# A four-fold column order in a fused convolution-and-attention block, with three smaller edits

## The chip, the cores and the metric

The kernel runs on one core of one Trainium2 chip. The time is the device time of one execution in microseconds. Before the change the median of three runs was 2451.59 us (2448.86 to 2452.62).

The core has five engines that run beside each other and wait for one another by semaphores: TensorE (PE, matrix products into PSUM), VectorE (DVE, arithmetic on one or two tensors), ScalarE (ACT, functions such as exp and SiLU, and copies), GpSimd (POOL, here small arithmetic, memsets and issuing transfers) and SyncE (SP, here only issuing transfers). PEld is PE's loading of weights. Each engine works its own list in order, so an instruction that waits holds up all that stand behind it. SBUF is the on-chip memory, PSUM the memory into which PE accumulates.

## The reference

Eight images x of 512 channels and 32 x 32 pixels, all in fp32:

```python
h = group_norm(x)                           # 32 groups
t = silu(bn(conv1x1(h, cv1_w)))             # 512 -> 512 channels
ys = [t[:, :256], t[:, 256:]]
for i in range(2):                          # two bottlenecks
    yi = ys[-1]
    z = silu(bn(conv3x3(yi, m_cv1_w[i])))
    q, k, v = conv1x1(z, m_qkv_w[i])        # 4 heads of 64 channels
    r = m_rw[i] + m_rh[i]                   # one term per column, one per row
    a = softmax(q.T @ (k + r) / 8)          # 1024 x 1024 per head
    z = silu(bn(conv1x1(a @ v, m_cv2_w[i])))
    ys.append(yi + z)
out = x + silu(bn(conv1x1(concat(ys), cv2_w)))   # 1024 -> 512 channels
```

Only the 3x3 convolution and the position term r depend on where a pixel lies. The 1x1 convolutions and the attention take the pixels in any order, as long as it is the same throughout.

## The kernel before, in words

Channels lie on the 128 partitions, pixels along the free axis. The images are worked in four pairs (the loop over p), a and b. For each pair the first bottleneck (n = 0) is done for a and b, then the second (n = 1), then the final 1x1 convolution for both; the first 1x1 convolution and the group norm of the next pair run in between. The last pair has no next one (more is false), and its last image takes a plain product (cv2) in place of the seven-product scheme (strassen).

A 3x3 convolution is done as a transform of tiles: four columns and four rows of output at a time. tiles_in (L422 to L485) makes the transformed input for one of three groups of rows i. It first combines rows into w_rows, which has 34 columns: the 32 of the image and a zero at each side (memsets L452 and L453 on POOL). It then combines columns. As four neighbouring columns belong to one tile, every column operation reads or writes every fourth element: d is the difference of columns two apart (L467), L470 to L474 take d by its place in a quad, L480 and L481 read w_rows at each fourth column. L483 and L484 finish the third output from the two tiles of L480 and L481. conv3x3 (L487 to L567) multiplies (L528), and in each of its six steps turns the products back: c_m on ACT (L533), c_t twice and c_e on DVE (L534 to L540), four operations that write each fourth column of c_r (L542 to L545), then sums over rows into z (L548 to L560) and SiLU (the helper at L398).

project_strassen (L704 to L800) makes q, k and v of one image in seven products. It adds r to k in add_r, as two DVE operations for each of four pieces, one with the column term broadcast over rows (L740), one with the row term (L741); the last two pieces are done by later() at the start of the attention. attention_fast (L802 to L976) runs 32 steps in four groups: logits on PE (L825), exp on ACT (L829), running sums on DVE (L843, L845), and the product with v on PE (L859). Other work is hung into it by the dictionary behind, keyed by group and pair of steps. The exponentials, the temporary tiles of project_strassen and tiles that tiles_in makes for the second bottleneck (v_new, stored to DRAM at L1551) share one ring of six buffers, tag "pt".

group_norm (L623 to L655) makes the norm of the next image in four stages inside the attention, at groups 1, 2, the middle of 2, and 3. Its last stage takes the reciprocal root on POOL (L599). Then, for the first pair (direct is true), POOL computes a shift and ACT applies scale and shift in eight pieces (L654); for later pairs DVE does it in four (L633).

strassen (L1084 to L1174) is the final 1x1 convolution. finish (L1131) takes one finished block: SiLU in place, an addition of x, which POOL's queue loaded ahead (residual, L1124 to L1129), on DVE (L1135), and a store from POOL's queue (L1136). The temporary tiles are a ring of four, tag "t".

The order of the work is not written out entirely: the framework places each instruction on its engine's list at the time at which its own estimate of costs has it ready, by program order among those that are ready; issue_after adds an order by hand. Transfers are placed on SP's and POOL's lists in the same way.

Of the kernel before, what the change touches and what calls it, by code (L numbers as in the profile page):

```python
# [47 lines left out]
ALU = mybir.AluOpType  # L48
# [13 lines left out]
def kernel(  # L62
# [112 lines left out]
    def load_bottleneck(n):  # L175
        nc.sync.dma_start(rw_sb[:, n], m_rw[n].rearrange("(k p) f -> p k f", p=P))
        nc.sync.dma_start(rh_sb[:, n], m_rh[n].rearrange("(k p) f -> p k f", p=P))
        nc.sync.dma_start(m2_sb[:, n], m_cv2_w[n].rearrange("(k p) o -> p k o", p=P))

# [157 lines left out]
    v_dram = [[tc.dram_tile([P, 2, 2 * P], F32, name=f"v{i}{cp}") for cp in range(3)] for i in range(NI)]  # L337
    y0_dram = [[tc.dram_tile([P, NM, HALF], F32, name=f"y0_{b}{h}") for h in range(NH)] for b in range(B)]
# [46 lines left out]
    def img2(ap):  # L385
        return ap.rearrange("p c (h w) -> p c h w", w=F)

# [6 lines left out]
    def stages(act, small, ps_big, ps_av, n_pt):  # L394
# [27 lines left out]
        def tiles_in(yp, put, is_=(0, 1, 2), ec=None):  # L422
# [16 lines left out]
            for i in is_:  # L439
# [23 lines left out]
                else:  # L463
                    stt(to[0], two(ec[1]), 0.25, two(g[:, :, 0]), ALU.mult, ALU.add)
                    stt(to[1], two(ec[0]), -4.0, two(g[:, :, 1]), ALU.mult, ALU.add)
                d = act.tile([P, 2 * NT * NM, F], F32, tag="acc", name="w_d", bufs=2)
                tt(d, e[:, :, 2 : F + 2], e[:, :, 0:F], ALU.subtract)  # L467
                quads = d.rearrange("p a (s j) -> p (a s) j", j=4)
                v05, v12, v34 = (put(i, cp) for cp in range(3))
                stt(  # L470
                    v05.rearrange("p c q -> p q c"), quads[:, :, 0:2], -4.0, quads[:, :, 2:4], ALU.mult, ALU.add
                )
                stt(v34[:, 0], quads[:, :, 1], 2.0, quads[:, :, 2], ALU.mult, ALU.add)
                stt(v34[:, 1], quads[:, :, 1], -2.0, quads[:, :, 2], ALU.mult, ALU.add)  # L474

                def each4(m):
                    return e[:, :, m : m + F - 3 : 4]

                ab = act.tile([P, 2, 2 * NT * NM, NT], F32, tag="h", name="w_ab", bufs=2)
                stt(ab[:, 0], each4(2), -4.0, each4(4), ALU.mult, ALU.add)  # L480
                stt(ab[:, 1], each4(1), -4.0, each4(3), ALU.mult, ALU.add)  # L481
# [5 lines left out]
        def conv3x3(n, vs, u_of, z, groups=G, summed=None):  # L487
# [10 lines left out]
            for oc in range(NM):  # L498
                dst = z[:, oc].rearrange("p g x -> p (g x)").rearrange("p (t r w) -> p r t w", r=4, w=F)
                for i in range(NI):  # L500
# [40 lines left out]
                    r = act.tile([P, 2, q, 4], F32, tag="acc", name="c3_r", bufs=2)  # L541
                    stt(r[..., 0], m[:, :, 2], -0.25, e[:, :, 0], ALU.mult, ALU.add)  # L542
                    stt(r[..., 1], m[:, :, 3], -0.5, m[:, :, 1], ALU.mult, ALU.add)
                    tt(r[..., 2], m[:, :, 0], m[:, :, 2], ALU.subtract)
# [78 lines left out]
        def group_norm(xts, on_act=False):  # L623
# [21 lines left out]
            if not on_act:  # L645
                yield apply(range(NX), gm, gr)
                return
# [1214 lines left out]
```

## Time and profile before

| | |
|---|---|
| median of three runs | 2451.59 us |
| profiled execution | 2449.15 us |
| its span, first to last instruction | 2447.6 us |
| PE busy | 2254.5 us (92%) |
| DVE busy | 1933.5 us (79%) |
| ACT busy | 1012.0 us (41%) |
| POOL busy | 178.4 us (7%) |
| mean granted PE clock | 0.97 |
| moved by transfers | 272.01 MB, mean 111 GB/s |

A row of a group reads: line, engine, operation, output and inputs by name, partitions x elements, count; then busy time in us and the mean of one in ns; then the engine's idle time just before them and what ended it. A row of a timeline reads: start in us, length in us, engine, line, what it is, and in brackets the idle time before it with what ended it. A row of waits reads: who, for whom, us in total, times, the longest.

The stages of a later pair, by start in us, for the second pair: 750 to 781 first 3x3 convolution; 804 to 862 attention of image a; 920 to 980 attention of b; 1003 to 1061 tiles and second 3x3 convolution; 1074 to 1131 and 1160 to 1218 the two attentions of the second bottleneck; 1218 to 1322 the final 1x1 convolution of both images.

### The profile page before, as it was taken

To read this page: it belongs to the slowest core of one execution; us is meant where nothing else is said; L and a number is where in the kernel's file an instruction comes from. 1 tells how busy PE (TensorE), PEld (TensorE's weight loads), DVE (VectorE), ACT (ScalarE), POOL (GpSimd) and SP (SyncE) were. 2 spreads that over 40 slices of the span, in tenths; PEclk is the share of its full clock that TensorE was granted. 3 is DMA by queue.
4 is the path that set the end of the run, shared out by engine and by line. 5 is a ranking of instruction groups with operands and counts; after the bars stand their busy time and mean duration, and the time that the engine had idled before them with its cause. 6 is when DMAs were issued, how large, how long until landed. Compare 5 with 4: busy or idle time off the path is not lost.

```text
span 2447.6 us, 40591 instructions
## 1 busy us (share of the span) xinstructions
PE 2254.5 (92%) x16378; PEld 1101.8 (45%) x16378; DVE 1933.5 (79%) x2766; ACT 1012.0 (41%) x1301; POOL 178.4 (7%) x409
## 2 busy tenths in 40 slices
PE   6698778899999999999999998989999996989998
PEld 2462333634347443654346443463444732363433
DVE  7987585987878879886896879898796878597653
ACT  4145244255413545246511455436521363425531
POOL 4101210000010000000011000000001000000002
PEclk9799889999999999999999999999999998999999
DMA  9531622621146141532036223351124502141113
GB/s 318 196 106 53 233 75 96 209 88 41 60 168 211 31 151 40 178 97 86 21 119 235 83 75 117 108 168 58 45 82 163 184 23 74 49 158 36 57 31 122
DMA packets 128644, 272.01 MB, mean 111 GB/s; under 512 B 34016, under 2 KB 63184, under 8 KB 127424
## 3 DMA queue, kind: packets, MB, share of 16 engines
q1 hardware_dynamic: 104368, 184.51, 23.6%
q0 software_dynamic: 24080, 84.82, 9.5%
q8 instruction: 131, 2.15, 0.4%
q14 instruction: 65, 0.53, 0.1%
HBM read 200.20 MB, written 69.07 MB: 110 GB/s over the span
## 4 chain that ended last, share of the span: by engine, by line
PE 63%; DVE 25%; issue 5%; DMA 3%; ACT 3%; POOL 1%; SPq 0%; DVEq 0%; POOLq 0%; ACTq 0%
PE av_ps L859 14%; PE l_ps L825 14%; PE c L1078 8%; PE c_new L1078 6%; PE p_ps L717 5%; PE m_ps L1058 4%; DVE acc L845 3%; PE c_ps L528 3%; PE ps L417 3%; PE x_ps L1189 2%; PE pv_ps L723 2%; PE s_ps L876 1%; DVE c_e L536 1%; DVE w_d L467 1%; PE p_ps L723 1%
## 5 line engine op out<-in xcount | busy, mean ns | idle before, releaser
L829 ACT ACTIVATE pt<-l_ps 128x1024 f32<-128x1024 f32 x512 | 496.4, 1025 | 370.2 <-PE l_ps L825 332.9
L845 DVE TENSOR_TENSOR acc<-acc,pt 128x1024 f32<-128x1024 f32 x384 | 469.7, 1223 | 97.5 <-ACT pt L829 73.7
L825 PE MATMUL l_ps<-q,kr 64*64 64x512 f32 x4096 | 493.3, 597 | 49.4 <-ACT pt L829 46.7
L859 PE MATMUL av_ps<-pt,vT 64*64 64x512 f32 x4096 | 494.3, 600 | 7.7 <-DVE z L867 6.6
L825 PEld LDWEIGHTS l_ps<-q,kr 64*64 64x64 f32 x4096 | 158.2, 134 | 323.3 <-issue 250.0
L859 PEld LDWEIGHTS av_ps<-pt,vT 64*64 64x64 f32 x4096 | 158.3, 135 | 286.8 <-issue 234.4
L528 PE MATMUL c_ps<-v_in,u 128*64 128x128 f32 x4320 | 245.9, 277 | 16.3 <-ACT c_m L533 16.3
L528 PEld LDWEIGHTS c_ps<-v_in,u 128*64 128x64 f32 x4320 | 242.9, 140 | 22.8 <-ACT c_m L533 17.4
L717 PE MATMUL p_ps<-t_z,sq 128*128 128x512 f32 x256 | 128.5, 619 | 19.4 <-DVE c_t L535 19.4
L1058 PE MATMUL m_ps<-z,m_sb 128*128 128x512 f32 x256 | 114.6, 600 | 8.9 <-DVE z L931 8.9
L533 ACT COPY c_m<-c_ps 128x512 f32<-128x512 f32 x48 | 28.0, 584 | 211.6 <-PE c_ps L528 83.8
L717 PE MATMUL p_ps<-z,sq 128*128 128x512 f32 x192 | 93.5, 618 | 17.2 <-ACT z L398 10.9
L843 DVE TENSOR_TENSOR acc<-pt 128x1024 f32<-128x1024 f32 x64 | 78.2, 1221 | 32.9 <-ACT pt L829 32.9
L931 DVE TENSOR_TENSOR z<-z,rs 128x512 f32<-128x512 f32 x64 | 44.1, 689 | 70.8 <-DMA rs<-r_dram 70.7
L398 ACT ACTIVATE t<-m_ps,bh,sh 128x512 f32<-128x512 f32 x64 | 47.0, 779 | 86.9 <-PE m_ps L1058 86.5
L1058 PEld LDWEIGHTS m_ps<-z,m_sb 128*128 128x128 f32 x256 | 48.7, 192 | 68.7 <-issue 56.8
L717 PEld LDWEIGHTS p_ps<-t_z,sq 128*128 128x128 f32 x256 | 45.4, 197 | 54.7 <-issue 52.3
L723 PEld LDWEIGHTS pv_ps<-sq,z 128*128 128x128 f32 x384 | 51.4, 200 | 37.8 <-issue 11.0
L723 PE MATMUL pv_ps<-sq,z 128*128 128x128 f32 x384 | 55.0, 288 | 13.3 <-DVE z L867 7.2
L467 DVE TENSOR_TENSOR w_d<-w_rows 128x1024 f32<-128x1024 f32 x48 | 58.8, 1225 | 3.6 <-DVE w_rows L462 0.5
L717 PEld LDWEIGHTS p_ps<-z,sq 128*128 128x128 f32 x192 | 34.2, 193 | 58.0 <-issue 35.2
L417 PE MATMUL ps<-x,w 128*128 128x512 f32 x128 | 57.0, 599 | 0.9 <-ACT y_half L398 0.9
(279 smaller groups left out, 3179.9 us busy)
## 6 DMA issues: line engine op xcount, KB each, us to landing
u<-u SPq DMA_DIRECT2D x135, 512.0 KB
sq<-sq SPq DMA_DIRECT2D x48, 384.0 KB
x_res<-in_x_dram POOLq DMA_DIRECT2D x63, 256.0 KB, 4.2
rs<-r_dram SPq DMA_DIRECT2D x120, 128.0 KB
x<-in_x_dram SPq DMA_DIRECT2D x28, 512.0 KB
y_in<-y SPq DMA_DIRECT2D x28, 512.0 KB
u<-u_new POOLq DMA_DIRECT2D x54, 256.0 KB, 2.9
v<-v_new POOLq DMA_DIRECT2D x36, 256.0 KB, 2.3
```

What stands on the lines that cost most here:

```text
L417: last_product[0] = nc.tensor.matmul(ps[:, half, :], w_of(k), rhs_of(k, half), start=(k == begin), stop=(k == end))
L467: tt(d, e[:, :, 2 : F + 2], e[:, :, 0:F], ALU.subtract)
L528: nc.tensor.matmul(to[o], us[cp][:, k, row, c, o], rhs, start=(k == 0), stop=(k == NM - 1),)
L717: nc.tensor.matmul(ps[:, o, :], w[:, o, :], rhs, start=not onto, stop=True, skip_group_check=onto)
L723: nc.tensor.matmul(v[:, ts(j, P)], rhs[:, ts(j, P)], w[:, 2, :], start=j == 0 and not onto, stop=True, skip_group_check=True,)
L825: nc.tensor.matmul(ps[kh * HD : (kh + 1) * HD, hd, :], kr[r, c, o : o + HD], q[r, c, ts(half, HALF)], start=True, stop=True,)
L829: exp = nc.scalar.activation(pt, ps, AF.Exp, scale=SCALE)
L843: return nc.vector.tensor_tensor(accs[g], pt[0], pt[1], ALU.add)
L845: ins = nc.vector.tensor_tensor(accs[g], accs[g], pt[i], ALU.add)
L859: nc.tensor.matmul(avs[g][hd * HD : (hd + 1) * HD, kh, :], vT[r, j, o : o + HD], pt[i][r, hd, :], start=(j == 0), stop=(j == NJ - 1),)
L1058: nc.tensor.matmul(pss[oc][:, half, :], m2_sb[:, n, k, ts(oc, P)], ao[:, k, ts(half, HALF)], start=(k == 0), stop=(k == NM - 1),)
L1078: nc.tensor.matmul(ps[:, o, :], w[:, k, ts(o, P)], rhs[part][:, c], start=(k == 0 and not onto), stop=(k == KB - 1), skip_group_check=onto,)
```

## The change

**Column order.** Between the first and the final 1x1 convolution the 32 columns of a row are stored by their remainder modulo four, remainder 3 first, eight of each. The first 1x1 convolution's SiLU and copies write that order (planes, natural), the final one's SiLU writes the natural order back (from_planes, by_slot). In tiles_in and conv3x3 each operation on every fourth column becomes one on runs of eight; L467 becomes two operations of half the size. The copies of L1199 into ypad are split in two.

**Position term.** r is summed once for each bottleneck by POOL at the start, stored in DRAM, and loaded on SP's queue into two "pt" tiles at each project_strassen; add_r has one addition.

**Residual.** In strassen, SiLU writes a fresh "t" tile, a transfer on POOL's queue adds x to it, and a second one stores it. The loads of x and the DVE additions go.

**Norm.** The last stage of group_norm is on POOL and ACT for all pairs.

**Last pair.** The tiles of image a's second convolution, made between projection and attention of b before, are made inside that attention, after the second pair of steps of groups 0, 1 and 2; their tiles take the tag "x" in place of "pt". In the plain cv2 the partial sum is added in place.

```diff
     def load_bottleneck(n):
-        nc.sync.dma_start(rw_sb[:, n], m_rw[n].rearrange("(k p) f -> p k f", p=P))
+        raw = act.tile([P, NM, F], F32, tag="t", name="rw_raw", bufs=4)
+        nc.sync.dma_start(raw, m_rw[n].rearrange("(k p) f -> p k f", p=P))
         nc.sync.dma_start(rh_sb[:, n], m_rh[n].rearrange("(k p) f -> p k f", p=P))
         nc.sync.dma_start(m2_sb[:, n], m_cv2_w[n].rearrange("(k p) o -> p k o", p=P))
+        nc.gpsimd.tensor_copy(planes(rw_sb[:, n]), natural(raw))
+        for c in range(NM):
+            for half in range(NH):
+                r = act.tile([P, ROWS, F], F32, tag="t", name="r_new", bufs=4)
+                nc.gpsimd.tensor_tensor(
+                    r, rw_sb[:, n, c].unsqueeze(1).to_broadcast([P, ROWS, F]),
+                    rh_sb[:, n, c, ts(half, ROWS)].unsqueeze(2).to_broadcast([P, ROWS, F]), ALU.add,
+                )
+                nc.gpsimd.dma_start(r_dram[n][c][:, ts(half, HALF)], r.rearrange("p h w -> p (h w)"))
...
+    def planes(ap):
+        a = ap.rearrange("p (h w) -> p h w", w=F) if len(ap.shape) == 2 else ap
+        return bass.AP(
+            tensor=a.tensor, offset=a[:, :, F - NT :].offset, ap=[a.ap[0], a.ap[1], [1, NT], [-NT, 4]]
+        )
+    def natural(ap):
+        a = ap.rearrange("p (h w) -> p h w", w=F) if len(ap.shape) == 2 else ap
+        return a.rearrange("p h (s j) -> p h s j", j=4)
+    def by_slot(ap):
+        a = ap.rearrange("p (h w) -> p h w", w=F) if len(ap.shape) == 2 else ap
+        return a.rearrange("p h (j s) -> p h j s", j=4)
+    def from_planes(ap):
+        a = ap.rearrange("p (h w) -> p h w", w=F) if len(ap.shape) == 2 else ap
+        return bass.AP(tensor=a.tensor, offset=a[:, :, 3:].offset, ap=[a.ap[0], a.ap[1], [-1, 4], [4, NT]])
...
-                d = act.tile([P, 2 * NT * NM, F], F32, tag="acc", name="w_d", bufs=2)
-                tt(d, e[:, :, 2 : F + 2], e[:, :, 0:F], ALU.subtract)
+                d = act.tile([P, 4, 2 * NT * NM * NT], F32, tag="acc", name="w_d", bufs=2)
...
+                tt(d_of(0), cols(M2, M3 - M2), cols(M0, M1 - M0), ALU.subtract)
+                tt(d_of(2), cols(M0 + 1, M1 - M0), cols(M2, M3 - M2), ALU.subtract)
...
-                stt(ab[:, 0], each4(2), -4.0, each4(4), ALU.mult, ALU.add)
-                stt(ab[:, 1], each4(1), -4.0, each4(3), ALU.mult, ALU.add)
+                stt(ab[:, 0], cols(M2), -4.0, cols(M0 + 1), ALU.mult, ALU.add)
+                stt(ab[:, 1], cols(M1), -4.0, cols(M3), ALU.mult, ALU.add)
...
-                    stt(r[..., 0], m[:, :, 2], -0.25, e[:, :, 0], ALU.mult, ALU.add)
+                    stt(r[:, :, :, 3], m2, -0.25, e0, ALU.mult, ALU.add)
...
-            if not on_act:
-                yield apply(range(NX), gm, gr)
-                return
...
+            rs = []
+            for c in range(NM):
+                rs.append(act.tile([P, HW], F32, tag="pt", name="r_in", bufs=n_pt))
+                nc.sync.dma_start(rs[c], r_dram[n][c])
             def add_r(c, half, src=None):
...
-                tt(dst, dst if src is None else img(src), rw, ALU.add)
-                return tt(dst, dst, rh, ALU.add)
+                dst = kr[:, c, ts(half, HALF)]
+                return tt(dst, dst if src is None else src, rs[c][:, ts(half, HALF)], ALU.add)
...
-            def finish(i, src, dst):
+            def finish(i, src):
                 o, half = blocks[i]
                 for at in range(2):
-                    silu(dst[:, at, :], src[:, at, :], bn_cv2 + 2 * o + at)
-                    tt(dst[:, at, :], dst[:, at, :], res[i][at], ALU.add)
-                    nc.gpsimd.dma_start(rows_of(out, i, at), dst[:, at, :])
-                if len(res) < len(blocks):
-                    residual()
+                    t = act.tile([P, HALF], F32, tag="t", name="c_out", bufs=4)
+                    silu(from_planes(t), by_slot(src[:, at, :]), bn_cv2 + 2 * o + at)
+                    nc.gpsimd.dma_start(t, rows_of(x, i, at), accum_op=ALU.add)
+                    nc.gpsimd.dma_start(rows_of(out, i, at), t)
...
-            v_new[i, cp] = t = act.tile([P, 2, 2 * P], F32, tag="pt", name="v_new", bufs=6)
+            tag, bufs = ("pt", 6) if more else ("x", NX)
+            v_new[i, cp] = t = act.tile([P, 2, 2 * P], F32, tag=tag, name="v_new", bufs=bufs)
...
-            for i in range(NI):
+            def tiles_later(i):
                 s.tiles_in(Y2[0], put_away, [i], ec)
                 store(i)
...
+            behind |= {(i, 2): (lambda i: lambda: tiles_later(i))(i) for i in range(NI)}
```

## The prediction

> **What bounds the kernel now.** I read the page first, then the groups by shape, the waits of TensorE (PE), busy time by stretch, and the timelines of PE, VectorE (DVE) and ScalarE (ACT) around the gaps.
>
> ```profile
> PE 2254.5 (92%) x16378; PEld 1101.8 (45%) x16378; DVE 1933.5 (79%) x2766; ACT 1012.0 (41%) x1301; POOL 178.4 (7%) x409
> ...
> PE 63%; DVE 25%; issue 5%; DMA 3%; ACT 3%; POOL 1%; SPq 0%; DVEq 0%; POOLq 0%; ACTq 0%
> ```
>
> PE is busy for 2254.5 of 2447.6 us. Nothing in the change removes a matmul, so at most the other 193 us can be won, and a faster DVE counts only where PE stands idle for it. DVE's 25% of the chain is the warning that such places exist. Busy time by stretch shows two kinds (columns: stretch, length, PE, PEld, DVE, ACT, POOL):
>
> ```profile
> 1003.00:1061.00 58.00, 50.30 (x624) 41.73 (x623) 56.20 (x97) 13.81 (x19) 0.45 (x4) 0.94 0.59 194
> ...
> 2294.00:2352.00 58.00, 57.58 (x538) 20.25 (x540) 46.55 (x51) 35.11 (x40) 0.00 (x0) 1.00 0.07 22
> ```
>
> The first is a 3x3 convolution of the second bottleneck: DVE is full, PE is not. The second is attention: PE is full, so saved DVE time is worth nothing there. PE's own waits name the causes, and its timeline the places:
>
> ```profile
> PE l_ps L825 <- ACT pt L829: 46.7, 9, 19.5
> PE c_ps L528 <- ACT c_m L533: 24.8, 6, 8.5
> PE p_ps L717 <- DVE c_t L535: 19.4, 8, 2.9
> ```
>
> ```profile
> 1025.34 25.48 PE L528 MATMUL c_ps<-v_in,u 128*64 128x128 f32 x416 [3.69 <-ACT c_m L533]
> ...
> 1055.87 1.95 PE L717 MATMUL p_ps<-t_z,sq 128*128 128x512 f32 x4 [2.24 <-DVE c_t L535]
> ...
> 1060.48 3.70 PE L717 MATMUL p_ps<-z,sq 128*128 128x512 f32 x8 [1.77 <-ACT z L398]
> ```
>
> Each is DVE at one remove: the copy L533 waits for a tile that L484 frees, and the SiLU L398 follows DVE's L560.
>
> **Part 1, the column order.** Four DVE operations of a tile pass and four of a convolution step now step over four columns:
>
> ```profile
> L467 DVE TENSOR_TENSOR w_d<-w_rows 128x1024 f32<-128x1024 f32 x48 | 58.8, 1225 | 3.6 <-DVE w_rows L462 0.5 <-POOL w_rows L453 0.2
> ...
> L470 DVE SCALAR_TENSOR_TENSOR v_in<-w_d 128x512 f32<-128x512 f32 x36 | 38.7, 1076 | 3.8 <-PE c L1078 3.8
> L542 DVE SCALAR_TENSOR_TENSOR c_r<-c_t,c_e 128x256 f32<-128x256 f32 x48 | 30.9, 644 | 0.0
> ...
> L480 DVE SCALAR_TENSOR_TENSOR w_ab<-w_rows 128x256 f32<-128x256 f32 x48 | 29.8, 622 | 0.0
> ...
> L483 DVE TENSOR_TENSOR v_in<-w_ab 128x256 f32<-128x256 f32 x36 | 15.2, 421 | 0.2
> ```
>
> 256 elements take 421 ns unstepped, 622 to 644 stepped. Back to back, DVE starts are closer than durations: 0.335 us for 256 plain elements (L483 to L484), 0.60 for 512, 1.14 for L467, 0.91 for L470, 0.52 for L473, L474, L480 and L481, 0.455 for L542 to L545. A tile pass goes from 1.14 + 0.91 + 4 x 0.52 = 4.13 to 0.60 x 2 (w_d is now two operations) + 0.60 + 4 x 0.335 = 3.14: -1.0 us, 48 times. A convolution step saves 4 x 0.12 = 0.48 us, 48 times.
>
> What reaches PE: at the start (70 to 146 us, DVE unbroken) six passes and six steps, 6 x 1.0 + 6 x 0.48 = -8.9 of PE's gaps at 83, 95, 110 and 146 us (4.29 + 7.64 + 8.47 + 2.54). In each of four second-bottleneck convolutions DVE is unbroken over three passes and six steps, -5.9 of about 7.7 (the gaps above: 3.69 + 2.24 + 1.77): -23.6. In the later three first-bottleneck ones, whose tiles were made under the final 1x1 work, five late steps, -2.4 each: -7.2. **Sum -40.** The cost from below is nothing; from above, runs of eight could still pay part of the step (+15), but 32-column runs at L467's row pitch of 34 pay nothing, so I take zero.
>
> [...] ACT now writes 8 x 4096 columns in steps of 32 bytes and as many in steps of 16[...]. No ACT row here is stepped. [...] priced with DVE's stepped write (0.86 ns an element), ACT gains 65536 x 0.86 = 56 us of work; by ACT's rows (776 ns whichever tile) nothing. Either way it lies under 6.87 us of matmuls per output tile; without that cover all 56 us would show. Only the last store feels it: +0.3. The eight 1024-wide copies of L1199 split in two cost ACT 8 x 0.16 us, under the same matmuls.
>
> **Part 2, position terms.** The second add goes: 64 x 0.60 us of DVE, mostly hidden; where attention starts with DVE behind (1.46 us before L876, 0.76 before L825, 1.20 before L723, twice each, more in the first pair) this and the shorter passes give **-8**. Added once, at 30 to 80 us, where DVE is full: on GpSimd (POOL) two small copies, 8 adds of 128x512 and 8 stores; the only wide POOL row, L312, is 0.35 us for 128 elements, so an estimate is 1.4 us an add, 11 in all. Behind them in POOL's order stand the filter stores, L599 to L614 of the second image's norm (ACT's L618 and PE wait for those) and the edge memsets L452. Between 0 and +8; **+2**, since POOL is idle more than half of that time.
>
> Also added: 32 loads of 512 KB on SP's queue and two of the six "pt" tiles for most of every projection. In the three first-bottleneck projections that share "pt" with v_new, ACT already waits for a slot (L749 at 905.66, L752 at 908.71, both on v<-v_new). Two slots later means about +1.6 us each. At the second-bottleneck ones the slots are free by 1131.2 us and the sum is wanted at 1142.79: hidden. If a load sits behind a filter load that waits (SP stood 19.88 us over L264 at 899.80), DVE stalls at the first add and PSUM stays full. 0 to +15; **+5**.
>
> **Part 3, residual.** 56 DVE adds go (0.60 each), but the final 1x1 stretches 646 to 750, 1217 to 1321 and 1791 to 1895 have no PE gap over 0.7 us: nothing gained. The output transfer now waits behind the accumulating one on POOL, with the edge memsets behind it. A plain L1128 load lands in 4.2 us; nothing here accumulates, so 4.2 (plain) to 8.4 us (an estimate: two reads). Piece 3's tile is wanted at 751.8 and free at 741.2 + 1.1 + landing + 2.9, so up to 6.6 us is hidden. 0 to +12; **+2**. At the end the last product's residual loads queue behind these pieces and its two "h" tiles come free later: 0 to +6; **+3**.
>
> **Part 4, norm on ACT.** The first pair has it already, the later pairs do not:
>
> ```profile
> 389.06 5.76 ACT L654 ACTIVATE x<-x,shift,gr 128x512 f32<-128x512 f32 x8 [5.00 <-POOL shift L650]
> ```
> ```profile
> 395.78 1.99 PE L825 MATMUL l_ps<-q,kr 64*64 64x512 f32 x8 [5.20 <-ACT pt L829]
> ```
> ```profile
> 855.47 2.99 DVE L633 TENSOR_SCALAR x<-x,gm,gr 128x1024 f32<-128x1024 f32 x4 [1.16 <-POOL gr L599]
> ```
>
> ACT stands 5.00 us for POOL's shift, then works 5.76; the exponentials queue behind it, and PE stops 5.20 us (7.17 the other time, with filter work in it). Beside the four DVE versions PE has no gap at all. So 4 x 5.2 = **+21**; 0 if ACT takes the exponentials first, 4 x 7.2 at worst. (Two small POOL operations more each time are inside those 5.00 us.) [...] DVE is not saturated there (46.55 of 58), so the row decides.
>
> **Part 5, last pair.** The tile work moves from before the attention into it:
>
> ```profile
> 2057.38 1.99 PE L825 MATMUL l_ps<-q,kr 64*64 64x512 f32 x8 [19.45 <-ACT pt L829]
> ```
>
> This stop goes. In its place each of three attention groups gets a lump of about 7 us: DVE then has 8 x 1.13 + 1.4 + 7 = 17.4 us against PE's 14.5, and v_new has only two free "x" tiles, so its third waits for a store landing (2.3 us). Late next: the running sums, then "pt" tiles. The six "pt" tiles are three pairs of 3.6 us, some 10 us of slack, which takes most of 3 x 2.9 and some store waits. Give back 0 to 12; I take 6: **-13**.
>
> **Sum.** -40 - 8 - 13 + 2 + 5 + 2 + 3 + 21 = -28 us on the profiled 2449.15 us (span 2447.6 and 1.55 around it), which lies 2.4 below the median of 2451.59. So 2451.6 - 28 = 2423.6, **2424 us**.
>
> **Rivals.** (a) The norm hides: -49, 2403 us. For: ACT is idle half of attention. Against: both cases in this trace stall. (b) The gaps close but re-form on the next wait, the SiLU or the filter loads (1.77 us before L717, SP's 19.88): half of parts 1 and 2, -4, 2448 us. (c) Slower: the position sums land late. Place: the add out of PSUM at L740, 16 projections, DVE in order behind it. For: the SP wait and the slot waits above. Against: 11 us of lead at 1131. Price 16 x d in place of the 5; it decides from d = (28 + 5) / 16 = 2.1 us, and d = 3 gives +15, 2467 us.
>
> **Chances.** Forecast 0.66, (a) 0.14, (b) 0.10, (c) 0.10. About 0.2% (4.9 us) is what a measurement can tell from no change. Forecast and (a), and 0.04 of (b), are faster, less 0.01: 0.83; same 0.07; slower 0.10. The forecast's own range is 2402 to 2441 from the ends above; 2392 to 2450 takes in (a), (b) and part of the unknown costs.
>
> **What would show it.** Right: stepped groups at 421 and 690 ns; gaps before c_ps and p_ps nearly gone; no 19 us stop; four new PE stops of about 5 us at the norm of the later pairs. Wrong: DVE waiting on the loaded sums, ACT on output tiles in the final stage, or those four stops absent.

## The result and the profile after

The changed kernel takes 2429.53 us in the median (2425.61 to 2433.19) against 2452.11 us of the kernel before beside it; the ratio is 0.9908, with a 95% interval of 0.9887 to 0.9929. That is 22.6 us less, where 28 were forecast (2424 us). The profiled execution took 2428.35 us, its span is 2426.9 us.

The page of the changed kernel (busy time with share and instructions; the chain that ended last, by engine):

```profile
PE 2253.8 (93%) x16378; PEld 1092.5 (45%) x16378; DVE 1776.7 (73%) x2678; ACT 1100.2 (45%) x1341; POOL 214.7 (9%) x435
...
PE 51%; DVE 21%; issue 17%; DMA 5%; ACT 4%; POOL 2%; SPq 0%; DVEq 0%; ACTq 0%; POOLq 0%
```

DVE lost 156.8 us of work, ACT gained 88.2, and PE's idle time fell by 20 us: most of DVE's saving was hidden, as the prediction said. The groups by shape show the stepped DVE operations at the plain durations that were forecast, and one that was not: ScalarE's stepped write.

```profile
L510 DVE TENSOR_TENSOR w_d<-w_rows 128x512 f32<-128x512 f32 x48 | 33.1, 690 | 8.6 <-POOL w_rows L483 5.8
...
L513 DVE SCALAR_TENSOR_TENSOR v_in<-w_d 128x512 f32<-128x512 f32 x36 | 24.7, 687 | 34.1 <-PE c L1111 34.1
...
L585 DVE SCALAR_TENSOR_TENSOR c_r<-c_t,c_e 128x256 f32<-128x256 f32 x48 | 20.3, 424 | 0.0
...
L517 DVE SCALAR_TENSOR_TENSOR w_ab<-w_rows 128x256 f32<-128x256 f32 x48 | 20.2, 421 | 0.1
...
L429 ACT ACTIVATE ypad<-ps,bh,sh 128x512 f32<-128x512 f32 x16 | 18.4, 1240 | 25.3 <-PE ps L448 22.3 <-DVE bh L1422 3.0
```

The same SiLU in the kernel before:

```profile
L398 ACT ACTIVATE ypad<-ps,bh,sh 128x512 f32<-128x512 f32 x16 | 11.7, 777 | 28.4 <-PE ps L417 25.4 <-DVE bh L1395 3.0
```

PE's waits and its timeline, at the places that the prediction showed:

```profile
PE l_ps L860 <- ACT pt L864: 43.0, 10, 7.2
PE p_ps L750 <- ACT u_z L784: 14.9, 3, 7.4
...
PE c_ps L565 <- ACT c_m L570: 10.2, 5, 7.7
...
PE p_ps L750 <- DVE c_t L572: 7.6, 7, 1.2
```
```profile
845.10 1.98 PE L860 MATMUL l_ps<-q,kr 64*64 64x512 f32 x8 [5.10 <-ACT pt L864]
...
1023.27 10.70 PE L565 MATMUL c_ps<-v_in,u 128*64 128x128 f32 x192 [0.63 <-ACT c_m L570]
...
1050.80 1.96 PE L750 MATMUL p_ps<-t_z,sq 128*128 128x512 f32 x4 [1.07 <-DVE c_t L572]
1054.83 3.70 PE L750 MATMUL p_ps<-z,sq 128*128 128x512 f32 x8 [1.18 <-ACT z L429]
```

The three gaps of a second-bottleneck convolution (3.69, 2.24 and 1.77 us before) are 0.63, 1.07 and 1.18 us, and four stops of 5.10 us are new. So the wait for exponentials has hardly shrunk (46.7 to 43.0 us) although the 19.45 us stop is gone, and a new row stands second: PE waits for u_z, whose tile ACT gets late.

Both traces hold 16378 matmuls in nearly the same order, so their starts can be compared one by one. The running difference, cut where it jumps, tells where time went; the list adds up, but for rounding, to the difference of the two spans (-20.7):

| place | predicted | in the traces |
|---|---|---|
| start and first pair, to 446 us of before | -6.9, and part of -8 for attention starts | -6.4 |
| four second-bottleneck convolutions | -23.6 | -7.5 - 6.6 - 6.6 - 6.5 = -27.2 |
| attention of the second bottleneck, first pair | part of -8 | -3.2 |
| three later first-bottleneck convolutions | -7.2 | -1.6 - 3.1 - 1.5 = -6.2 |
| the norm on ScalarE, four times | +21 | +7.8 + 7.9 + 7.2 + 7.9 = +30.8 |
| projections with loaded sums, second and third pair, with the attention start behind each | part of +5 and of -8 | +2.9 + 2.4 = +5.3 |
| last pair, tiles moved | -13 | -21.5 + 5.2 = -16.3 |
| residual, first final stage | +2 | +1.0 |
| last pair's end | 0 | -0.6 |
| after the last matmul | +3 | +2.2 |

Most rows are near their forecast. The norm is half as dear again, though its stop has the forecast length. Why is in the stretches around it (columns: stretch, length, busy time of PE, PEld, DVE, ACT and POOL with instructions, granted clock, DMA share, GB/s):

```profile
835.00:840.00 5.00, 4.99 (x52) 2.10 (x44) 1.63 (x3) 1.61 (x3) 1.47 (x3) 1.00 0.03 5
840.00:845.00 5.00, 0.00 (x0) 0.00 (x0) 0.00 (x0) 5.00 (x8) 0.00 (x0) 0.81 0.00 0
845.00:850.00 5.00, 4.90 (x24) 1.54 (x28) 4.82 (x6) 4.61 (x7) 0.00 (x0) 0.51 0.02 1
850.00:855.00 5.00, 5.00 (x27) 1.87 (x20) 5.00 (x9) 1.83 (x3) 0.00 (x0) 1.00 0.20 52
```

For 5 us ACT does the eight norm operations and PE nothing; in the next 5 us PE runs at a granted clock of 0.51 and takes up 24 matmuls, where about 47 of this kind would go at the pace just before the stop (16 in 1.71 us). That is another 2.1 to 2.8 us for each stop, which the prediction's working, in idle time alone, did not see.

The start has a second surprise. DVE's timeline has operations that last several times their usual 0.42 us, and POOL's shows what runs then:

```profile
58.23 2.75 DVE L378 TENSOR_TENSOR u_new<-u_new,ypad 128x256 f32<-128x256 f32 x1
...
65.28 2.48 DVE L377 TENSOR_TENSOR u_new<-ypad 128x256 f32<-128x256 f32 x1
```
```profile
58.63 2.06 POOL L184 TENSOR_TENSOR r_new<-rw_sb,rh_sb 128x512 f32<-128x512 f32 x2
...
65.41 2.06 POOL L184 TENSOR_TENSOR r_new<-rw_sb,rh_sb 128x512 f32<-128x512 f32 x2
```

A third (1.94 us instead of 0.56) is at 38.37 us. DVE's first tile operation starts at 76.13 us instead of 70.29: 5.84 us, the 1.38 + 2.33 + 2.06 us of the three. The shorter passes win some 9 us behind it, and little of that is left.

### The profile page after: what moved, and what is told of

Its sections match the earlier page's. It is cut to its first block, busy times and chain, and to the rows that moved or that the text cites. A ratio compares the mean times of both kernels' runs of the same rounds, so it can differ in the third digit from the quotient of the medians.

```text
span 2426.9 us, 40682 instructions
## 1 busy us (share of the span) xinstructions
PE 2253.8 (93%) x16378; PEld 1092.5 (45%) x16378; DVE 1776.7 (73%) x2678; ACT 1100.2 (45%) x1341; POOL 214.7 (9%) x435
## 4 chain that ended last, share of the span: by engine, by line
PE 51%; DVE 21%; issue 17%; DMA 5%; ACT 4%; POOL 2%; SPq 0%; DVEq 0%; ACTq 0%; POOLq 0%
PE av_ps L894 12%; PE l_ps L860 12%; PE p_ps L750 5%; PE c L1111 5%; PE m_ps L1091 3%; PE c_new L1111 3%; PE ps L448 3%; DVE acc L880 3%; PE x_ps L1211 2%; PE c_ps L565 2%; DMA c_out<-in_x_dram 2%; PE pv_ps L756 2%; ACT x L687 1%; ACT pt L864 1%; DVE c_e L573 1%
## 5 line engine op out<-in xcount | busy, mean ns | idle before, releaser
L894 PE MATMUL av_ps<-pt,vT 64*64 64x512 f32 x4096 | 500.1, 606 | 11.2 <-DVE z L902 7.6
L565 PE MATMUL c_ps<-v_in,u 128*64 128x128 f32 x4320 | 239.9, 273 | 5.2 <-issue 2.7
L565 PEld LDWEIGHTS c_ps<-v_in,u 128*64 128x64 f32 x4320 | 235.8, 137 | 12.8 <-issue 12.8
L1161 POOL DMA_DIRECT2D c_out<-in_x_dram x56 | 49.6, 967 | 307.8 <-ACT c_out L429 303.2
L902 DVE TENSOR_TENSOR z<-av_ps,z 128x512 f32<-128x512 f32 x64 | 44.1, 689 | 24.3 <-ACT z L901 24.3
```

The costliest lines, as they stand in the source:

```text
L565: nc.tensor.matmul(to[o], us[cp][:, k, row, c, o], rhs, start=(k == 0), stop=(k == NM - 1),)
L894: nc.tensor.matmul(avs[g][hd * HD : (hd + 1) * HD, kh, :], vT[r, j, o : o + HD], pt[i][r, hd, :], start=(j == 0), stop=(j == NJ - 1),)
L1161: nc.gpsimd.dma_start(t, rows_of(x, i, at), accum_op=ALU.add)
```

## The experiments

Unless said otherwise each kernel is the changed one with one edit, and differences are taken from its 2429.53 us. The kernel before took 2450.83 to 2452.99 us beside them. Intervals are about 0.2% wide to each side, so medians that differ by less than some 6 us are not told apart by their times; there the matched matmuls are given, from one execution each.

### Norm's last step back on DVE (part 4 undone)

```
+            if not on_act:
+                for c in range(NX):
+                    nc.vector.tensor_scalar(xts[c], xts[c], gm[:, c : c + 1], gr[:, c : c + 1], ALU.subtract, ALU.mult)
+                yield
+                return
...
-            norm = s.group_norm(xs)
+            norm = s.group_norm(xs, direct)
```

> The changed kernel with the norm's last step of the second and third pair back on DVE (part 4 undone). In the trace of the changed kernel each of the four new stops (5.10 us) is followed by 8 matmuls per 1.71 us instead of 0.86, at a granted clock of 0.51 in 845 to 850 us, and by the time the two traces run in step again 7.2 to 7.9 us are lost, not 5.1. Theory: a stop costs its length and about 2.6 us at the halved clock: -31 us against the changed kernel, about 2399 us. First rival: only the stop's length counts, -20 us, about 2409 us. Second rival: DVE, which gets 8 x 1.5 us of work per pair back, is late elsewhere, and nothing is won: 2425 to 2430 us.

Measured: 2402.93 us, ratio 0.9799 (0.9774 to 0.9824): -26.6 us. The stretches and DVE's timeline of this kernel:

```profile
833.00:838.00 5.00, 5.00 (x56) 2.42 (x52) 3.74 (x7) 2.03 (x3) 1.04 (x1) 1.00 0.03 5
838.00:843.00 5.00, 5.00 (x49) 2.24 (x41) 4.90 (x6) 4.36 (x5) 0.00 (x0) 1.00 0.02 1
```
```profile
836.33 2.98 DVE L683 TENSOR_SCALAR x<-x,gm,gr 128x1024 f32<-128x1024 f32 x4 [1.16 <-POOL gr L642]
```

DVE does in 2.98 us what took ACT 5.75, and PE neither stops nor slows. The time lies between the theory (-31) and the first rival (-20) and does not tell them apart; the places do. Matmul by matmul the four give back 7.8, 7.9, 6.9 and 7.9 us, 30.5 in all, where the length of the stops alone would be 20.4. So the theory holds at the places. Some 4 us are lost again elsewhere in this execution, most of it at stops of 2.7 to 4.2 us that slow the clock here more than in the changed kernel's trace (behind one stop of 2.69 us it is 0.50 here and 1.00 there, last section). The second rival falls.

### Position terms in two adds (part 2 undone)

```
-                return tt(dst, dst if src is None else src, rs[c][:, ts(half, HALF)], ALU.add)
+                tt(dst, dst if src is None else img(src), rw, ALU.add)
+                return tt(dst, dst, rh, ALU.add)
```
(and without POOL's sums, their stores and their loads; the second bottleneck's terms are loaded behind the first tile passes again)

> The changed kernel with the position terms added in two steps to every product again (part 2 undone; no sums on POOL, no stores or loads of them). Theory: three DVE operations at 38, 58 and 65 us took 1.94, 2.75 and 2.48 us instead of 0.42 to 0.56 while POOL ran the adds; without them the head is 5.8 us earlier, and the three projections that share their tiles with the loads are 7 us faster together; the attention starts lose about 8 us again: -5 us, about 2425 us. First rival, the sizes of the prediction: +8 - 2 - 5 = +1 us, about 2430 us. Second rival: the second add of each product is on the path everywhere, 64 x 0.6 us less what attention hides, +15 us, about 2445 us.

Measured: 2426.67 us, ratio 0.9898 (0.9875 to 0.9922): -2.9 us, which the times do not tell from nothing; the second rival (+15) falls. The matched matmuls show the two sides: the start is 5.9 us earlier and no DVE operation there is over 1.3 us; by 184 us all but 0.2 of it is lost again, 2.0 in the first convolution and the rest where the first attention starts; the projections at 902 and 1484 us win 4.2 and 3.5 us in one jump and keep winning 1 to 2.5 behind it; later attention starts lose 1 to 3 us each. PE ends 3.3 us earlier. Part 2 is gains and losses of about the same size, not a gain.

The jump at 902 us is PE behind ACT's first copy there, in the changed kernel (PE's and ACT's timelines):

```profile
902.72 6.29 PE L750 MATMUL p_ps<-z,sq 128*128 128x512 f32 x8 [4.07 <-ACT u_z L784]
```
```profile
901.66 1.01 ACT L784 COPY u_z<-p_ps 128x1024 f32<-128x1024 f32 x1 [5.00 <-DMA v<-v_new]
```

u_z needs a "pt" tile, and with two of the six taken by the loaded sums it waits for the store of a v_new tile. That is the slot wait that the prediction named. With two adds this stop is absent. The row of u_z in PE's waits has three such stops: 7.38 us at 299 us, in the first pair, where the two-add run has two of 0.90 and 4.09 us, then this one, and 3.43 us at 1484 us.

### Tiles of the last pair before the attention (part 5 undone)

```
-            def tiles_later(i):
+            for i in range(NI):
                 s.tiles_in(Y2[0], put_away, [i], ec)
                 store(i)
...
-            behind |= {(i, 2): (lambda i: lambda: tiles_later(i))(i) for i in range(NI)}
```

(the tag "x" and the sum in place of the plain cv2 stay as they are)

> The changed kernel with the last pair's tile passes back between the projection and the attention (part 5 undone). Theory: the stop before the exponentials comes back with the halved clock behind it, 21.4 us, and the 5.2 us that the attention gave back go: +16 us, about 2446 us. Rival, the size of the prediction: +13 us, about 2442 us. Second rival: the faster passes (3.14 us instead of 4.13) have made the stop 9 us shorter by themselves, and only +8 us come back: about 2438 us.

Measured: 2440.56 us, ratio 0.9960 (0.9949 to 0.9972): +11.0 us. PE's timeline:

```profile
2059.28 1.98 PE L894 MATMUL av_ps<-pt,vT 64*64 64x512 f32 x8 [13.18 <-ACT pt L864]
```

The stop is 13.18 us, not 19.45: the faster passes alone take 6.3 us of it. Moving them away is worth the other 13.2 and the halved clock behind it (0.50 in the 2.5 us after it), 15.9 us at this place, less 4.7 that the attention gives back. The truth lies between the rival of the prediction's size and the second rival; the theory (+16) counted the 6.3 us twice.

### Columns in natural order (part 1 undone)

```
     def planes(ap):
-        return bass.AP(..., ap=[a.ap[0], a.ap[1], [1, NT], [-NT, 4]])
+        return natural(ap)
```
(and the tile pass and the convolution step as in the kernel before)

> The changed kernel with the columns in their natural order (part 1 undone, parts 2 to 5 kept): DVE's eight stepped operations are back, and ScalarE writes unstepped. Theory: the sum of the places in the two traces, 8.8 us at the start, 27.4 at the four second-bottleneck convolutions and 6 at the three later first-bottleneck ones come back: +42 us, about 2472 us. First rival: ScalarE's stepped writes (1240 ns instead of 777) cost something on the path, and so the return is smaller, +25 us, about 2455 us. Second rival: the gaps are taken over by other waits, +20 us or less, 2450 us or below.

Measured: 2479.48 us, ratio 1.0117 (1.0091 to 1.0144): +50.0 us. Parts 2 to 5 alone make the kernel 28 us slower than it was. PE's timeline has two of the three gaps again, longer than those left by the change by 3.05 and 1.88 us:

```profile
1047.65 24.73 PE L553 MATMUL c_ps<-v_in,u 128*64 128x128 f32 x416 [3.68 <-ACT c_m L558]
1078.13 3.08 PE L732 MATMUL p_ps<-t_z,sq 128*128 128x512 f32 x4 [2.95 <-DVE c_t L560]
```

By place: 8 us at the start, 3.1 around the first pair's second projection (260 to 325 us), 6.6 to 7.8 in each second-bottleneck convolution, 2.4 to 4.0 in each later first-bottleneck one, 1.2 at the projection at 902 us and 2.2 in the last pair's attention, whose tile passes are longer again; some 3 us come off in between. At the projection the stop for u_z is 8.23 us here instead of 4.07, and yet little is lost: the changed kernel runs 10.2 us of that stretch at half the clock, this one 6.8. Part 1 is worth more than its forecast 40 mainly because the convolutions give back more than was counted for them. ACT's writes are back at 774 ns, and no stretch of the matched matmuls is faster for it by more than 2 us: what the stepped writes cost on the path is small. Both rivals fall.

### Without the residual (bounds part 3)

```
-                    nc.gpsimd.dma_start(t, rows_of(x, i, at), accum_op=ALU.add)
```

(it leaves x out of the outputs of strassen)

> The changed kernel without the accumulating transfer (the residual is left out of the outputs of the Strassen 1x1 stages, so the output differs; ScalarE's tile is stored at once). It bounds what part 3 costs: an output tile comes free 5.3 us earlier and POOL has 56 issues of 0.97 us less. Theory: hidden but for the last store and one wait of about 1 us at 768 us: -2 to -3 us, about 2427 us. Rival: output tiles that come free late (ScalarE waits 16.8 us for them) and POOL's edge memsets behind the transfers (DVE waits 13.6 us for them) reach PE: -8 us or more, 2421 us or below.

Measured: 2425.09 us, ratio 0.9893 (0.9874 to 0.9913): -4.4 us, which the times alone do not tell from nothing. Three of its four executions took 2424.7 to 2425.4 us; the profiled one, 2430.35 us, has one stop of 3.20 us at 2247.8 where the changed kernel's has 0.45. The matched matmuls give 0.9 us back at 753 us and 1.4 at 769 us, both in the convolution behind the first final stage, and from the last matmul to the end it takes 2.8 us less. The theory fits. The times do not exclude the rival's 8 us, but the traces have no place for it. What hides the transfer is shown by its row and by POOL's wait for it:

```profile
c_out<-in_x_dram POOLq DMA_DIRECT2D x56, 256.0 KB, 5.3
```
```profile
POOL out_dram L1162 <- DMA c_out<-in_x_dram: 158.0, 56, 7.5
```

It lands in 5.3 us, between the two ends that were set (4.2 and 8.4), and POOL stands on it for 158 us. Of what is queued behind, the edge memsets, DVE's w_d waits for some (5.8 us in the row L510 above).

### The norm in pieces on ScalarE

First try, one tile (two operations) per step of the attention, in all three pairs:

```
             for c in range(NX):
                 ...
-            yield
+                yield
...
-        NORMS = (1, 2, (2, 2), 3)
+        NORMS = (1, 2, (2, 2), 3, (3, 1), (3, 2), (3, 3))
```

> The changed kernel with the norm's last step still on ScalarE, but one tile (two operations, 1.44 us) in each of the last four steps of the attention instead of eight operations in one lump; in all three pairs that have it, the first too. Theory: the stop comes from the lump, which is longer than the exponentials that PE has in hand; a step has 3.5 us of PE and 2 x 1.02 us of exponentials, so 1.44 us fit. The four new stops (7.3 us each, 29 in all) and the first pair's two (7.15 and 5.19 us and the halved clock behind each, some 17 us) go: -46 us against the changed kernel, about 2384 us. First rival: ScalarE is full in these four steps (3.48 of 3.5 us) and each slips by about 1 us, 24 in all: -22 us, about 2407 us. Second rival: a pair's 5.8 us of norm cost PE their full length wherever they stand on ScalarE: 0, about 2430 us.

Measured: 2424.17 us, ratio 0.9892 (0.9873 to 0.9912): -5.4 us, just under what the times tell apart. ACT's and PE's timelines say why the forecast failed:

```profile
836.11 1.52 ACT L687 ACTIVATE x<-x,shift,gr 128x512 f32<-128x512 f32 x2 [3.84 <-POOL shift L683]
...
840.05 3.62 ACT L687 ACTIVATE x<-x,shift,gr 128x512 f32<-128x512 f32 x5
843.57 1.91 ACT L864 ACTIVATE pt<-l_ps 128x1024 f32<-128x1024 f32 x2
```
```profile
844.63 3.59 PE L894 MATMUL av_ps<-pt,vT 64*64 64x512 f32 x16 [3.24 <-ACT pt L864]
```

The order worked out for ACT put five of the eight side by side again, ahead of the last two exponentials, so this run did not test what it was meant to. A second try starts from the kernel with the sums pinned into the first attention (2393.32 us, described below), whose later norms are on DVE. It has the statistics earlier and each piece pinned behind its exponential:

```
+                    with ExitStack() as order:
+                        for exp in last_exp:
+                            order.enter_context(tc.issue_after(exp.ins))
...
-        NORMS = (1, 2, (2, 2), 3)
+        NORMS = (1, (1, 2), (1, 3), (2, 1), (2, 3), 3, (3, 1), (3, 2))
```

> The same, but the norm's last step on ScalarE in all three pairs, its statistics one to two groups earlier, so that POOL's shift is there in time, and two operations (1.44 us) pinned behind the exponentials of each of the last four steps; in the earlier spread run ScalarE's order had put five of the eight side by side again and PE stopped 3.24 us. Theory: with the pieces truly apart no stop over 1.5 us is left: the second and third pair as with DVE (0), the first pair's two stops (7.15 and 5.18 us, with the halved clock 7 to 10 each) go, -15 us, about 2371 us. First rival: a step's 3.48 us of ScalarE against 3.43 us of PE leave no room for the other copies (0.6 and 0.4 us), each norm loses 2 us: about 2383 us. Second rival: 5.8 us of norm cost PE their full length wherever they stand: 4 x 7.3 come back, about 2415 us.

Measured: 2383.76 us, ratio 0.9723 (0.9707 to 0.9739), against 2393.32 of its base: -9.6 us. ACT now alternates. The second fence has the largest row of PE's waits in this kernel; its base has this wait once, for 2.0 us:

```profile
821.65 1.55 ACT L695 ACTIVATE x<-x,shift,gr 128x512 f32<-128x512 f32 x2
823.48 1.94 ACT L877 ACTIVATE pt<-l_ps 128x1024 f32<-128x1024 f32 x2 [0.27 <-PE l_ps L873]
825.30 1.51 ACT L695 ACTIVATE x<-x,shift,gr 128x512 f32<-128x512 f32 x2
826.91 1.94 ACT L877 ACTIVATE pt<-l_ps 128x1024 f32<-128x1024 f32 x2
```
```profile
PE gm_ps L624 <- DVE mv L618: 16.1, 7, 4.2
```

PE runs through all of it: its timeline has no idle time from 806 to 835 us. The same work on the same engine costs nothing at that spot: it is the lump, not ScalarE's total, that stops PE, and the second rival falls. The earlier statistics bring their own wait, though: PE's small gm matmul now comes to DVE's mean too soon and waits 1.7 to 2.1 us in each of the four later places, where the matched matmuls lose 2.1 to 2.8. A loss of 2 us for each norm is what the first rival named, but not by this cause: no stop for ACT is found there. Counted from the base, the total lies between the theory (-15) and that rival (-3). In the first pair 15.1 us are won by 395 us.

### POOL's sums elsewhere

```
-    for n in range(N):
-        load_bottleneck(n)
+    load_bottleneck(0)
...
+    load_bottleneck(1)
```
(the second call stands behind the first tile passes)

> The changed kernel with POOL's sums of the second bottleneck's position terms made after the first tile passes (in the first attention) instead of beside the filters; the first bottleneck's stay. Theory: a DVE operation with two inputs from SBUF stands still while POOL adds; two of the three long DVE operations (2.75 and 2.48 us instead of 0.42) are at these sums, so the head is 4.4 us earlier, and in the attention DVE has room: -4.4 us, about 2425 us. First rival: the head's delay comes from the stores and loads, not from POOL's adds; it only moves: -1 us, about 2428 us. Second rival: in the attention the running sums stand still in their turn, and PE waits for them: +2 us, about 2431 us.

Measured: 2434.16 us, ratio 0.9934 (0.9909 to 0.9960): +4.6 us. It settles nothing about the start: POOL's order, worked out anew, left the sums beside the filters (63 to 73 us), and DVE has four long operations there (1.96, 2.52, 1.59, 1.60 us), 5.7 us over their usual time, as before. The 4.6 us are not told apart from nothing by the times; the matched matmuls have 1.3 of them by 150 us and 2.2 between 1800 and 2000 us, and the cause stays open.

The mixed kernel has two adds in the first bottleneck, sums in the second alone, and the norm of the later pairs on DVE:

```
-        for c in range(NM):
+        for c in range(NM if n else 0):
...
+                if n:
                     return tt(dst, dst if src is None else src, rs[c][:, ts(half, HALF)], ALU.add)
```

> The changed kernel with the norm's last step of the second and third pair on DVE, the first bottleneck's position terms in two adds (no sums, no loads in its projections), and the second bottleneck's summed once, after the first tile passes. Theory: norm -26.6 (measured alone), no POOL adds beside the filters -5.8, the three first-bottleneck projections without the slot waits -2 each net of the later attention start, the second bottleneck's gain (3.2 us at 601 us) kept: -38 us, about 2391 us. First rival: the parts only share gaps, and the norm's is all: -27 us, about 2403 us. Second rival: DVE, with norm and second add back, is late at the attention starts of the first bottleneck as in the kernel before (1.46 and 0.76 us, twice): -33 us, about 2396 us.

Measured: 2388.64 us, ratio 0.9744 (0.9725 to 0.9763): -40.9 us, 14 less than with the norm alone. The parts add up. Its matched matmuls: the stretches around the projections at 902 and 1484 us win 5.3 and 4.4, the norms most of the rest; of 2.9 us at the start (one long DVE operation is left, 2.90 us at 59.99 us) 1.6 remain by 191 us.

With those sums pinned into the first attention:

> The kernel of the mixed run (norm of the second and third pair on DVE, first bottleneck in two adds) with POOL's sums of the second bottleneck now pinned behind the second attention group's second step, about 190 us, instead of beside the filters, where POOL's order left them before. Theory: the one long DVE operation that the mixed run still has at the start (2.90 us instead of 0.55, at 59.99 us, as POOL adds) goes, and in the attention the stall falls on DVE while PE has work in hand: -2 us against the mixed run, about 2386 us, and the long operations are then found behind 190 us. Rival: the running sums stand still there and PE waits for them: +2 us, about 2391 us.

Measured: 2393.32 us, ratio 0.9752 (0.9736 to 0.9768); PE ends 4.8 us later than in the mixed kernel, though the ratios are not told apart. Again the sums did not go where they were meant to. POOL's and DVE's timelines:

```profile
107.41 5.10 POOL L186 TENSOR_TENSOR r_new<-rw_sb,rh_sb 128x512 f32<-128x512 f32 x2
```
```profile
110.26 1.35 DVE L512 TENSOR_TENSOR w_d<-w_rows 128x512 f32<-128x512 f32 x1
111.53 1.53 DVE L513 TENSOR_TENSOR w_d<-w_rows 128x512 f32<-128x512 f32 x1
```

Two of them ran beside a tile pass, where DVE has no gap at all. This time POOL stood still as well: 5.10 us for a pair that takes 2.06 elsewhere. The other pair, at 156.17 us, made no DVE operation long.

### The best version

The base of the last run, with the norm on DVE in the first pair too:

```
-            norm = s.group_norm(xs, direct)
+            norm = s.group_norm(xs, False)
```

> The same as the first of these three, but the norm's last step on DVE in the first pair too, whose attention has the second bottleneck's filter work on DVE. Theory: the two stops there go, and DVE is late by its 3 us instead: -15 + 2 x 3 = -9 us, about 2377 us. First rival: DVE is full there (8.9 tenths) and every microsecond of it is on the path: 2 x 3 us and the stops stay for the filter work, 0, about 2386 us. Second rival: nothing is late, -15 us, about 2371 us.

Measured: 2380.59 us, ratio 0.9702 (0.9686 to 0.9718), 12.7 us less than its base, between the theory (-9) and the second rival (-15).

And the mixed kernel with it:

> The mixed run (first bottleneck in two adds, second summed once by POOL at the start) with the norm's last step on DVE in all three pairs. Theory: the first pair's gain of the run before (12.6 us at the last matmul) adds to the mixed run's 2388.6 us, since the places are apart: about 2376 us. Rival: the place of POOL's sums makes no difference and the two are equal: about 2381 us. Second rival: the first attention, which now has POOL's filter stores, the norm and the filters on DVE, is late without the sums pinned into it: 2385 us or more.

Measured: 2380.16 us, ratio 0.9716 (0.9702 to 0.9729); nearest to the rival's 2381 us, though the theory's 2376 is not told from it by the times. So no effect of the place of POOL's sums is shown between these two. In the traces they differ on the way: at 58 us this one is some 5 us behind the run before, and by its end 2.2 ahead. Both beat both kernels: some 71 us less than before and 49 less than the change. The page of the last one:

```profile
PE 2239.6 (94%) x16378; PEld 1095.4 (46%) x16378; DVE 1810.7 (76%) x2734; ACT 1066.5 (45%) x1293; POOL 205.9 (9%) x415
```

PE is busy 14.2 us less than in the changed kernel with the same matmuls: so much of the gain is matmuls at a higher granted clock (0.982 in the mean against 0.973), not idle time.

## Why the prediction was right, and where it was off

**The whole.** 2424 us was forecast and 2429.53 came, faster as said, inside the forecast's own range of 2402 to 2441. The reasons held step by step in the list above; the 5 to 6 us between are the norm's halved clock (+10 in the traces) and POOL's sums (+4), less what the convolutions and the last pair brought beyond their terms (3 to 4 each). That these errors offset each other is luck. One bound was wrong: "at most the other 193 us can be won" takes PE's busy time as fixed, and the best version has 14.2 us less of it than the changed kernel with the same matmuls.

**Part 1.** Mechanism right, size 40 against 50 when it is undone. The mis-sized terms are those of the convolutions, 5.9 us against 6.6 to 7.8 in the second bottleneck and 2.4 against 2.4 to 4.0 in the first: the gaps of 3.7 us have slow matmuls behind them (a granted clock of 0.50 to 0.69 in the 2.5 us after them in the natural-order run), which closing them gave back too. The 5 us in the attention stages of the first and the last pair were not in the sum. For ScalarE the prediction had two estimates: 56 us of work if ACT's stepped write costs 0.86 ns an element as DVE's does, and none by ACT's rows, which had no stepped write. The first was near: 1240 against 777 ns is 0.90 ns for each of 512 elements, and of ACT's 88 us more some 23 are the norm's 32 new operations at 0.72 us start to start, which leaves 65 against the estimate of 56. That it is hidden either way was right as well, and the natural-order run shows it.

**Part 2.** -8, +2 and +5 were forecast, -1 in all; undoing it wins 2.9 us, so the part may cost that much, which the times do not tell from -1. The term that failed is the +2 for POOL's sums: 5.84 us. It rested on POOL being idle half of the time and priced only what waits behind POOL in its queue; what the changed kernel's trace shows is DVE operations of 1.94, 2.75 and 2.48 us beside POOL's adds, where 0.42 to 0.56 are usual. The +5 for the slots was low as well: not a delay of about 1.6 us at each of three projections, but one stop at ACT's first copy, of 4.07 and 3.43 us in the later two and of 7.38 in the first pair, where two adds have 4.99. The attention starts, which lose 1 to 3 us each when the part is undone, pay for most of both.

**Part 3.** +2 and +3 forecast; +1.0 and +2.2 in the traces, and 4.4 us come back without the transfer.

**Part 4.** The stop was forecast at 5.2 us and is 5.10, four times. The term was the idle time and left out the slow clock behind it: +21 against 26.6 when undone and 30.8 in the traces. The row that was used for it (395.78 us of before) had that slow stretch right behind it, at a granted clock of 0.66 from 395 to 400 us. The 2.98 us of work that leave DVE with each norm are no gain: with them back, PE is busy all through 833 to 843 us at a granted clock of 1.00. The row decided rightly.

**Part 5.** -13 forecast, 11.0 when undone. Two errors nearly cancel: the 19.45 us stop was priced whole, though part 1 takes 6.3 of it, and the slow clock behind it (2.7 us) was left out.

**The rivals.** (a), that the norm hides, would have been right for its work but not for its lump: in pieces it does hide, but for the wait that the earlier statistics bring. (b) is excluded by the gaps. (c), sums that land late, did not happen. The answer for the adds' tile gives DVE's only wait before them, on ACT and not on the load:

```profile
its engine sat idle before it (us, times) until:
  ACT q L794: 30.8, 16
```

## What to carry to other kernels

Price a stop of the matmul engine at its length and the slow clock behind it (5.10 us of idle time cost 7.2 to 7.9 here), and read the granted clock in the stretch after each stop before pricing the next one. In these traces a lone stop under 1.8 us left the granted clock at 1.00, one over 4 us always lowered it (from 5.10 us on to 0.50), and between them it went either way (1.00 and 0.50 behind 2.69 us). Moving work to an idle engine is decided by the longest piece that stands in that engine's queue ahead of something urgent, not by its busy share: eight operations side by side cost 7 to 8 us, the same eight between exponentials nothing themselves. And a queue's idle time is no promise that its work is free, since POOL's adds were paid by DVE (5.8 us at the start of the changed kernel).

## What the runs showed of the hardware

**The granted clock after a stop.** Behind 160 us, in the kernels before and after and in four of the experiments: stops of 0.50 to 1.80 us leave the clock at 1.00 in the 2.5 us after them, unless another stop came a few us before; those between 1.9 and 4.2 us leave it anywhere from 1.00 to 0.50; all from 5.10 to 19.45 us leave it at 0.50.

The clock records of the 14 traces (one execution of each kernel) show what goes with it in between. Each trace has a grid of 3.41 us steps, and its stretches at 0.50 begin and end on it; behind 160 us there are 209 of them, 195 of which last one step or two. The grid lies differently in each trace (the step edges below at 1129.83 and 1112.03 us are 5.2 steps apart). A full-rate step that was followed by a slow one had PE busy for at most 0.45 of it, one that was followed by another full-rate step for at least 0.41. The way back from a slow step came where PE was busy for at least 0.79 of it and did not come where it was for at most 0.82. (The ends of matmuls are modelled, so these shares are rough.) One and the same stop of 2.69 us falls on either side of that. The steps are, in the changed kernel (stop up to 1131.73 us) and in the one with the norm on DVE (up to 1116.07 us):

```profile
1129.83:1133.25 3.42, 1.52 (x10) 1.19 (x10) 1.89 (x3) 2.62 (x6) 0.00 (x0) 1.00 0.89 369
1133.25:1136.66 3.41, 3.41 (x18) 2.14 (x17) 0.20 (x1) 2.00 (x4) 0.00 (x0) 1.00 0.20 52
```
```profile
1112.03:1115.44 3.41, 1.35 (x10) 0.30 (x2) 0.94 (x3) 3.38 (x6) 1.07 (x2) 1.00 1.03 419
1115.44:1118.86 3.42, 2.79 (x10) 2.25 (x11) 1.78 (x3) 1.63 (x3) 0.00 (x0) 0.50 0.57 231
```

PE was busy for 0.44 of the first step in one and for 0.40 in the other. As an estimate from these shares, a stop can halve the clock from about 2.0 us on (0.59 of 3.41), if it falls into one step, and must from about 4.0 us on, wherever it falls. It also gives the norm's price: its stop at 840 us leaves PE busy for 0.30 us of the step from 839.69 to 843.11 us, two steps at 0.50 follow, to 849.94, and the 4.84 us of them behind PE's restart at 845.10 cost 2.4 us, within the 2.1 to 2.8 found above. No step had to be idle throughout for a slow one to follow (PE was busy for 0.40 of the one at 1112.03 us), nor busy throughout for the way back (0.79).

**POOL's add and DVE.** In the twelve kernels with POOL's adds of 128x512, 25 DVE operations took 1.35 to 2.90 us where 0.42 to 0.69 are usual; each has two inputs in SBUF and each overlaps such an add. Five bn_stats of DVE, with one input, took 0.64 to 0.68 us each beside such adds (34 to 40 us of the changed kernel) and 0.67 elsewhere. In four experiments (the norm on DVE, the tiles before the attention, natural order, no residual) it is POOL's operation that is long at 58 us: one add takes 2.25 to 2.27 us instead of 1.04, and the five two-input operations of DVE beside it have their usual 0.41 to 0.42. In the kernel before and in the two-add run, which have none of these adds, no such operation is long.

**The accumulating transfer.** 256 KB land in 5.3 us where the plain load took 4.2, and one issue takes POOL 0.97 us where the plain one took 0.54:

```profile
L1161 POOL DMA_DIRECT2D c_out<-in_x_dram x56 | 49.6, 967 | 307.8 <-ACT c_out L429 303.2
```
